# New-value gates of two GRU cells: from full-height halves to four quarters of the TensorE array

## The chip, the cores and the metric

The kernel runs on one core of a Trainium2 chip. The metric is device time of one execution in microseconds; the figure given is a median over runs. A profile of one execution, taken by the hardware profiler, shows every instruction of every engine. The engines are PE (TensorE, the matrix multiplier, whose weight loads are listed apart as PEld), DVE (VectorE), ACT (ScalarE), POOL (GpSimd) and SP (SyncE, which here issues the loads of the adjacency matrix).

## The reference

Four graph layers work on 3327 nodes with 64 features and a dense-stored adjacency matrix `adj` of 3327 x 3327 fp32. The layer that matters here is the first one: two gated cells one after the other, each with a product by `adj`.

```python
def _ggc(x, adj, W, wih, whh, bih, bhh):
    m = adj @ (x @ W)
    gi = m @ wih.T + bih
    gh = x @ whh.T + bhh
    i_r, i_z, i_n = jnp.split(gi, 3, axis=-1)
    h_r, h_z, h_n = jnp.split(gh, 3, axis=-1)
    r = jax.nn.sigmoid(i_r + h_r)
    z = jax.nn.sigmoid(i_z + h_z)
    n = jnp.tanh(i_n + r * h_n)
    return (1.0 - z) * n + z * x
...
h = jax.nn.relu(_ggc(x, adj, W1, wih1, whh1, bih1, bhh1))
return jax.nn.relu(_ggc(h, adj, W2, wih2, whh2, bih2, bhh2))
```

The new value `n` needs two products that cannot be added up in the matrix multiplier: the state part `h_n`, which is multiplied by `r`, and the message part `i_n`. For `r` and `z` the two parts are simply added.

The layers after it (a decayed neighbour sum, three hops with the squared matrix, two hops with tanh) are not touched.

## The kernel before

**Nodes and chunks.** The nodes are padded to 3328 and split into two halves `s = 0, 1` of 13 blocks of 128. Four chunks of nodes hold 3, 3, 3 and 4 of these blocks (of both halves): widths of 384, 384, 384 and 512 columns. Chunks 0 and 1 form group 0, chunks 2 and 3 group 1. A tile is 128 rows of the transposed adjacency matrix over the columns of one group, 768 or 896 KB, loaded by SP into one of 20 slots.

**Hops.** There are eight products by the matrix ("hops", k = 0 to 7). `alone(0, 0)` runs hop 0 for group 0 over all 26 tiles and counts the nonzero entries of every tile on the way (`count`, L598, from a mask that DVE makes at L517). Then `joint(1, 0)` runs hops 0 and 1 for group 1, `joint(0, 1)` hops 1 and 2 for group 0, and so on. `run()` writes out the order of all instructions by hand; the framework adds no reordering. The hop itself is L697: for each tile and chunk two matmuls, one for each half of the nodes, of 128 rows and 64 columns of weights. So the array is used as two column halves side by side, everywhere in the kernel.

**Tasks between.** Work that isn't a hop is a generator. It yields the time that it would like to let pass, and `spend` lets it go on when so much hop work has been issued; `take` may push other tasks on when no PSUM bank is free. `after_0` and `after_1` run the gated cell (`gru`) when a chunk's sum of hop 0 or 1 is complete.

**A cell.** `both[c]` holds two slabs of 128 partitions for a chunk. In slab `s` the partitions `upper(s)` hold the message `m` of half `s` (copied from PSUM by `evacuate_stacked`, L942 to L946), and the other 64 hold the state. `cells[:, cell, s, g]` holds the weights for slab `s` and gate `g`, stacked in the same order: g = 0 and 1 are `r` and `z`, with both parts; g = 2 is the state part of the new value, `nh`, with zeros in the message's rows; g = 3 is the message part, `ni`, with zeros in the state's rows. `gate(g)` (L1007) runs two matmuls of 128 rows and 64 columns, whose outputs are the two partition halves of one PSUM bank. ACT takes the sigmoids of `r` and `z` (L1012); DVE then forms `(nh + bias) * r` (L1017) and adds `ni` (L1019), ACT takes the tanh (L1028), and DVE blends (L1032 to L1034).

**The first cell's state part.** In the first cell the state is known from the start. `ahead_of_cell(c)` makes `nh` of chunk c with two matmuls (L217), and ACT copies it (L218) into half a tile slot (`rooms`), where it stays until `gru` reads it at L1017. `more_constants` calls it four times, 4 us of hop work apart, while the tiles of `alone(0, 0)` come in. `gru` then runs three gates in the first cell and four in the second.

Of the kernel before, what the change touches and what calls it, by code (L numbers as in the profile page):

```python
# [9 lines left out]
F32 = mybir.dt.float32  # L10
# [36 lines left out]
P = 128  # L47
# [5 lines left out]
CH = [(0, 3), (3, 6), (6, 9), (9, 13), (3, 5), (5, 6)]  # L53
NC = 4
PARTS = (4, 5)
CWM = 512
GROUPS = [(0, 1), (2, 3)]
# [39 lines left out]
def upper(n):  # L97
    return slice(n * D, (n + 1) * D)
# [3 lines left out]
def kernel(  # L102
# [9 lines left out]
    nc = tc.nc  # L112
# [16 lines left out]
    cells = const.tile([P, 2, 2, 4, D], F32, name="cells")  # L129
# [3 lines left out]
    both = [const.tile([P, 2, (b1 - b0) * P], F32, name=f"both{c}") for c, (b0, b1) in enumerate(CH[:NC])]  # L133
    both += [both[1][:, :, (CH[c][0] - CH[1][0]) * P:(CH[c][1] - CH[1][0]) * P] for c in PARTS]
    bcol = const.tile([P, NBIAS], F32, name="bcol")
# [29 lines left out]
    def unfold_cell(cell):  # L165

        n = 3 * D + (NBIAS if cell == 0 else 0)
        i, ps = take()
        for h in range(2):
            nc.tensor.matmul(ps[upper(h), :n], ident[:, :D], stage[:, 4 * D:4 * D + n], start=True, stop=True)  # L170
        v = ps[:, :3 * D].rearrange("p (g f) -> p g f", f=D)
        for h in range(2):
            nc.vector.tensor_copy(cells[upper(1 - h), cell, h, 0:3], v[upper(1 - h)])
        if cell == 0:
            nc.vector.tensor_copy(bcol, ps[:, 3 * D:n])
        give(i)
# [24 lines left out]
            nc.vector.tensor_copy(cells[upper(h), cell, h, 3], v[upper(h), 2])  # L201
        give(i)

    ahead = {}
    rooms = [None, None]

    def ahead_of_cell(c):

        finish(c)
        g = c // 2  # L210
        if rooms[g] is None:
            rooms[g] = Mask(sum(width(ch) for ch in GROUPS[g]))
        w0 = (CH[c][0] - CH[GROUPS[g][0]][0]) * P
        ahead[c] = rooms[g].view.rearrange("p s w -> p (s w)").bitcast(F32)[:, w0:w0 + width(c)]
        i, ps = take()
        for s in range(2):
            nc.tensor.matmul(ps[upper(1 - s), :width(c)], cells[:, 0, s, 2, :], both[c][:, s], start=True, stop=True)  # L217
        nc.scalar.copy(ahead[c], ps[:, :width(c)])  # L218
        give(i)

    def fold_hops():

        i, ps = take()
# [28 lines left out]
    def more_constants():  # L252
        nc.gpsimd.memset(cells, 0.0)
        for c in range(NC):
            for h in range(2):
                nc.gpsimd.memset(both[c][upper(h), h], 0.0)  # L256
        nc.gpsimd.memset(bd, 0.0)
        yield 4.5
        unfold_cell(0)
        yield 1.3  # L260

        full = work.tile([P, P], BF16, name="t2")
        nc.gpsimd.memset(full, -TWO7)
        nc.gpsimd.affine_select(out=tri, in_=full, pattern=[[-1, P]], compare_op=ALU.is_gt, fill=0.0,
                                base=0, channel_multiplier=1)
        nc.gpsimd.affine_select(out=tri, in_=tri, pattern=[[-1, P]], compare_op=ALU.not_equal, fill=TWO7 * TWO7,
                                base=0, channel_multiplier=1)
        nc.gpsimd.memset(tri[:, P - 1:P], 0.0)
        nc.gpsimd.memset(bitsb, BITS)
        nc.gpsimd.memset(lasty, 0.0)  # L270
        nc.gpsimd.memset(sel, 0.0)
        wide = work.tile([P, P], F32, name="t2")
        nc.gpsimd.memset(wide, 0.0)

        for h in range(2):
            nc.vector.tensor_tensor(sel[:, h, :NQ], ident[:, h * D:h * D + NQ],
                                    ident[:, h * D + LATE:h * D + LATE + NQ], ALU.add)
        for i, (bi, bh) in enumerate(((BI1, BH1), (BI2, BH2))):
            nc.vector.tensor_add(bsum[:, i], bcol[:, bi:bi + 2], bcol[:, bh:bh + 2])

        nc.vector.tensor_scalar(wide[0:D], wide[0:D], bcol[0:D, BL1:BL1 + 1], None, op0=ALU.add)
        yield 9.75
        i, ps = take()
        mm(ps[:, :D], wide, ident[:, :D])
        nc.vector.tensor_copy(brow[:, 3], ps[:, :D])
        give(i)
        yield 1.5
        have.add("row")
        yield from fold_cell(0)
        have.add(0)  # L290
        for c in range(NC):
            yield 4.0
            ahead_of_cell(c)
        yield 35.25
        load_cell(1)
        yield 20.0
        unfold_cell(1)
        yield from fold_cell(1)
        have.add(1)
        yield 10.4  # L300
        for h in range(2):
            nc.sync.dma_start(out=bd[upper(h), :, upper(h)], in_=weights[:, WL1:WL3])
            for i in range(2):
                nc.sync.dma_start(out=w3[upper(h), :, i], in_=weights[:, WL3 + (h + i) % 2:NW:2])
        yield 8.0
        nc.sync.dma_start(
            out=brow[:, 0:3],
            in_=bass.AP(tensor=bias_rows.tensor, offset=bias_rows.offset, ap=[[0, P], [D, 3], [1, D]]),
        )
        yield 21.0  # L310
        yield from fold_hops()
        have.add("hops")


    def blocks(c):
        return CH[c][1] - CH[c][0]

    def width(c):
        return blocks(c) * P

    def mm(out, lhsT, rhs, start=True, stop=True):


        for h in range(2):
            hs = slice(h * D, (h + 1) * D)
            nc.tensor.matmul(out[hs], lhsT[:, hs], rhs, start=start, stop=stop)  # L326
# [8 lines left out]
    def take(sums=False, either=True):  # L335


        either = either and not sums
        pool = idle_sums if sums else idle_temps
        if either and idle_sums and (not pool or released[idle_sums[0]] < released[pool[0]]):  # L340
            pool = idle_sums
        for c in list(tasks):
            if not pool and c not in running:
                advance(c)
        i = pool.popleft()
        return i, banks[i]

    def give(i):
        released[i] = max(released) + 1
        (idle_sums if i < 4 else idle_temps).append(i)  # L350
# [21 lines left out]
    def advance(c):  # L372
        running.add(c)
        try:
            tasks[c][1] = next(tasks[c][0])
        except StopIteration:
            del tasks[c]
        running.discard(c)
# [6 lines left out]
    def finish(c):  # L385
        while c in tasks:
            advance(c)
# [607 lines left out]
    def gru(acc, c, bi, bh, cell, pace=1.0):  # L995

        assert cell in have
        w = width(c)
        evacuate_stacked(acc, c, on_scalar=cell == 0)
        yield 0.8 * pace  # L1000
        at = dead.popleft()
        r, z, d = (slots[at].rearrange("p s w -> p (s w)")[:, i * CWM:i * CWM + w] for i in range(3))

        def gate(g):
            i, ps = take()
            for s in range(2):
                nc.tensor.matmul(ps[upper(1 - s), :w], cells[:, cell, s, g, :], both[c][:, s], start=True, stop=True)  # L1007
            return i, ps

        for g, v in enumerate((r, z)):  # L1010
            i, ps = gate(g)
            nc.scalar.activation(v, ps[:, :w], AF.Sigmoid, bias=bsum[:, cell, g:g + 1])  # L1012
            give(i)
        nh = None if cell == 0 else gate(2)
        ni = gate(3)
        yield 0.75 * pace
        nc.vector.scalar_tensor_tensor(r, ahead[c] if nh is None else nh[1][:, :w], bcol[:, bh + 2:bh + 3], r,  # L1017
                                       op0=ALU.add, op1=ALU.mult)
        nc.vector.tensor_tensor(r, r, ni[1][:, :w], ALU.add)  # L1019
        give(ni[0])  # L1020
        if nh is not None:
            give(nh[0])
        else:
            del ahead[c]
            if not any(ch in ahead for ch in GROUPS[c // 2]):
                rooms[c // 2].free()
        yield 1.2 * pace
        nc.scalar.activation(r, r, AF.Tanh, bias=bcol[:, bi + 2:bi + 3])  # L1028
        yield 0.8 * pace
        for s in range(2):  # L1030
            u = upper(1 - s)
            nc.vector.tensor_tensor(d[u], both[c][u, s], r[u], ALU.subtract)  # L1032
        nc.vector.tensor_tensor(d, d, z, ALU.mult)
        nc.vector.tensor_tensor(d, d, r, ALU.add)  # L1034
        if cell == 0:
            nc.vector.tensor_scalar(both[c][upper(0), 1], d[upper(0)], 0.0, None, op0=ALU.max)
            if c in GROUPS[1]:
                turned[c] = nodes(c)
                turn(turned[c], c, 1)
        yield 2.4 * pace  # L1040
        if cell == 0:
            nc.scalar.activation(both[c][upper(1), 0], d[upper(1)], AF.Relu)
            yield 0.6 * pace
        return at, d
# [181 lines left out]
```

## Time and profile before

| | |
|---|---|
| median of 3 runs | 685.08 us (684.77 to 685.13) |
| the profiled execution | 684.89 us, of which its span is 683.2 us |
| matmul instructions on PE | 4984 records, all of 64 weight columns |
| the ahead sums (L217) | 16 matmul records from 39.3 to 53.9 us |
| the gates (L1007) | 112 matmul records from 60.8 to 208.9 us |
| ACT's copies of the ahead sums (L218) | 4, of 479 to 587 ns |
| loads from memory | 201.30 MB, 295 GB/s on average over the span |

The span runs from the first to the last instruction, and the rest of the profiled execution's time lies around it. A matmul of fp32 data shows as two records, one for each pass, each with its own weight load. In a timeline several records of one kind are merged into one line: start, length from the first start to the last end, engine, line, operation, names, shapes, number, and in brackets how long the engine had been idle and what ended that. Matmul ends are modelled, so lengths overlap: what a matmul costs is the distance from its start to the start of what follows.

### The profile page before, as it was taken

To read this page: it belongs to the slowest core of one execution; us is meant where nothing else is said; L and a number is where in the kernel's file an instruction comes from. 1 tells how busy PE (TensorE), PEld (TensorE's weight loads), DVE (VectorE), ACT (ScalarE), POOL (GpSimd) and SP (SyncE) were. 2 spreads that over 40 slices of the span, in tenths; PEclk is the share of its full clock that TensorE was granted. 3 is DMA by queue.
4 is the path that set the end of the run, shared out by engine and by line. 5 is a ranking of instruction groups with operands and counts; after the bars stand their busy time and mean duration, and the time that the engine had idled before them with its cause. 6 is when DMAs were issued, how large, how long until landed. Compare 5 with 4: busy or idle time off the path is not lost.

```text
span 683.2 us, 12502 instructions
## 1 busy us (share of the span) xinstructions
PE 672.1 (98%) x4984; PEld 369.8 (54%) x4984; DVE 390.5 (57%) x839; ACT 272.4 (40%) x427; POOL 76.9 (11%) x115
## 2 busy tenths in 40 slices
PE   7999999999999999999999999999999999999997
PEld 5776444445558886566455554444444443344464
DVE  7954898739998999666542108215483893005101
ACT  1014000312148988999987009522366510000101
POOL 5400000002660504021000000000010000000000
PEclk9999999999999999999999999999999999999999
DMA  9999998299889615783999379954997399918991
GB/s 340 401 401 405 405 405 308 78 344 399 279 270 339 244 56 164 274 307 119 358 400 324 124 281 406 406 231 141 401 375 252 123 408 404 405 46 313 397 404 45
DMA packets 68693, 201.30 MB, mean 295 GB/s; under 512 B 7244, under 2 KB 8372, under 8 KB 68636
## 3 DMA queue, kind: packets, MB, share of 16 engines
q1 hardware_dynamic: 65724, 199.08, 78.0%
q10 hardware_dynamic: 736, 1.23, 0.5%
q8 instruction: 39, 0.64, 0.4%
q0 software_dynamic: 2176, 0.20, 0.2%
q14 instruction: 18, 0.15, 0.1%
HBM read 199.45 MB, written 0.85 MB: 293 GB/s over the span
## 4 chain that ended last, share of the span: by engine, by line
PE 94%; DVE 2%; POOL 2%; issue 0%; DMA 0%; ACT 0%; DVEq 0%; ACTq 0%; POOLq 0%
PE sum L697 81%; PE temp L326 5%; PE temp L1007 2%; PE sum L326 1%; PE temp L598 1%; PE sum L1007 1%; PE temp L886 1%; PE temp L611 1%; POOL both L256 1%; DVE e L573 0%; POOL st L966 0%; DMA xs<-in_x 0%; DVE adj L517 0%; DVE st L963 0%; DVE y L962 0%
## 5 line engine op out<-in xcount | busy, mean ns | idle before, releaser
L697 PE MATMUL sum<-adj,y 128*64 128x384 f32 (+3 forms) x3016 | 533.0, 501 | 0.0
L697 PEld LDWEIGHTS sum<-adj,y 128*64 128x64 f32 x3016 | 242.7, 137 | 241.4 <-issue 151.3
L481 ACT ACTIVATE adj<-adj 128x768 f32<-128x768 f32 (+1 forms) x169 | 138.1, 890 | 27.0 <-DMA adj<-in_adjT 13.7
L517 DVE TENSOR_SCALAR adj<-adj 128x768 f16<-128x768 f32 (+2 forms) x156 | 86.2, 594 | 9.8 <-DMA adj<-in_adjT 6.7
L697 PE MATMUL sum<-e,both 128*64 128x384 bf16 (+1 forms) x624 | 73.9, 339 | 0.0
L575 ACT ACTIVATE e<-temp,bitsb 128x384 int16<-128x384 f32 (+1 forms) x113 | 63.6, 605 | 13.2 <-PE temp L326 11.3
L942 ACT COPY both<-sum 64x384 f32<-64x384 f32 (+3 forms) x17 | 8.1, 478 | 145.4 <-PE sum L697 145.3
L483 DVE TENSOR_TENSOR adj<-adj 128x768 f32<-128x768 f32 (+1 forms) x39 | 37.7, 1013 | 42.9 <-DMA adj<-in_adjT 31.8
L946 DVE COPY both<-sum 64x384 f32<-64x384 f32 (+3 forms) x11 | 6.2, 561 | 97.9 <-ACT both L942 96.7
L937 DVE STREAM_TRANSPOSE y<-t 32x96 f32<-32x96 f32 (+1 forms) x128 | 35.6, 278 | 40.8 <-ACT t L922 39.2
L966 POOL TENSOR_TENSOR st<-st,mhalf 128x6 f32<-128x6 f32 (+1 forms) x16 | 25.5, 1592 | 296.9 <-DVE st L964 296.9
L697 PEld LDWEIGHTS <-both 128*64 128x64 bf16 x624 | 44.6, 110 | 13.3 <-issue 3.5
L523 POOL DMA_DIRECT2D adj<-totals x52 | 32.0, 617 | 165.4 <-DVE adj L512 128.6
L326 PE MATMUL temp<-adj,tri 128*64 128x384 bf16 (+1 forms) x316 | 49.0, 341 | 0.1
L573 DVE TENSOR_SCALAR e<-temp 128x384 int16<-128x384 f32 (+1 forms) x45 | 27.7, 618 | 19.1 <-ACT e L575 12.0
L326 PEld LDWEIGHTS <-tri 128*64 128x64 bf16 x416 | 30.3, 110 | 13.7 <-issue 7.8
L915 DVE STREAM_TRANSPOSE both<-y 32x96 f32<-32x96 f32 (+1 forms) x128 | 35.6, 278 | 2.5
L512 DVE SCALAR_TENSOR_TENSOR adj<-adj,adj 128x896 f16<-128x896 f32 x26 | 28.4, 1092 | 0.9
L922 ACT ACTIVATE t<-sum,hopcol 128x384 f32<-128x384 f32 (+1 forms) x8 | 4.9, 608 | 51.8 <-PE sum L697 49.0
L575 ACT ACTIVATE e<-sum,bitsb 128x384 int16<-128x384 f32 (+1 forms) x35 | 20.5, 593 | 5.4 <-PE sum L326 3.8
L598 PE MATMUL temp<-adj,behind 128*64 128x384 f16 x104 | 18.4, 327 | 2.1 <-DVE adj L517 1.9
L326 PE MATMUL sum<-adj,tri 128*64 128x384 bf16 (+1 forms) x100 | 18.5, 335 | 0.9 <-DVE e L573 0.7
(153 smaller groups left out, 360.0 us busy)
## 6 DMA issues: line engine op xcount, KB each, us to landing
adj<-in_adjT SPq DMA_DIRECT2D x130, 768.0 KB, 8.7
adj<-in_adjT SPq DMA_DIRECT2D x104, 896.0 KB, 12.9
xs<-in_x ACTq DMA_DIRECT2D x1, 448.0 KB
adj<-totals POOLq DMA_DIRECT2D x26, 3.0 KB, 4.6
adj<-totals POOLq DMA_DIRECT2D x26, 3.5 KB, 2.9
out<-xs ACTq DMA_DIRECT2D x1, 256.0 KB
xs<-in_x ACTq DMA_DIRECT2D x1, 192.0 KB, 3.1
xs<-in_x SPq DMA_DIRECT2D x1, 192.0 KB
```

The costliest lines, as they stand in the source:

```text
L326: nc.tensor.matmul(out[hs], lhsT[:, hs], rhs, start=start, stop=stop)
L481: nc.scalar.activation(sq, v, AF.Square)
L483: nc.vector.tensor_tensor(sq, v, v, ALU.mult)
L512: nc.vector.scalar_tensor_tensor(t.mask.ones, t.view()[:, 1], 0.0, t.mask.ones, op0=ALU.not_equal, op1=ALU.add)
L517: nc.vector.tensor_scalar(to[:rows, half], t.view()[:rows, half], 0.0, None, op0=ALU.not_equal)
L523: nc.gpsimd.dma_start(out=t.mask.view[P - 1:P], in_=totals[t.g][t.q:t.q + D + 1:D, :])
L573: nc.vector.tensor_scalar(wide[:, s], ps[:, :w], BITS, 0.0, op0=ALU.add, op1=ALU.max)
L575: nc.scalar.activation(wide[:, s], ps[:, :w], AF.Relu, bias=bitsb)
L697: nc.tensor.matmul(acc[h][1][h * D:(h + 1) * D, :w], yq[h], rhs[h], start=first and n == 0, stop=last and n == len(terms) - 1)
L915: nc.vector.transpose(to[at:at + 32, :, q], h[q * 32:(q + 1) * 32, :, s, f * 32:(f + 1) * 32])
L937: nc.vector.transpose(yk[q * 32:(q + 1) * 32, :, s, f * 32:(f + 1) * 32], v[at:at + 32, :, q])
L966: nc.gpsimd.tensor_tensor(st[:, 3, :n], st[:, 2, :n], mhalf[:, :n], ALU.pow)
```

## The change

The function `ahead_of_cell` and its rooms go, with the four calls. `more_constants` lets 16 us pass in their place, as before. In `gru` both cells now make `nh` and `ni` at the same place, in two PSUM banks, with four matmuls that take only the 64 rows that hold nonzero weights:

```diff
-        for c in range(NC):
-            yield 4.0
-            ahead_of_cell(c)
+        yield 16.0
...
-        nh = None if cell == 0 else gate(2)
-        ni = gate(3)
+        nh, ni = take(), take()
+        for s in range(2):
+            for (_, ps), g, rows in ((nh, 2, upper(1 - s)), (ni, 3, upper(s))):
+                nc.tensor.matmul(ps[upper(1 - s), :w], cells[rows, cell, s, g, :], both[c][rows, s],
+                                 start=True, stop=True)
         yield 0.75 * pace
-        nc.vector.scalar_tensor_tensor(r, ahead[c] if nh is None else nh[1][:, :w], bcol[:, bh + 2:bh + 3], r,
+        nc.vector.scalar_tensor_tensor(r, nh[1][:, :w], bcol[:, bh + 2:bh + 3], r,
                                        op0=ALU.add, op1=ALU.mult)
         nc.vector.tensor_tensor(r, r, ni[1][:, :w], ALU.add)
         give(ni[0])
-        if nh is not None:
-            give(nh[0])
-        else:
-            del ahead[c]
-            if not any(ch in ahead for ch in GROUPS[c // 2]):
-                rooms[c // 2].free()
+        give(nh[0])
```

The four matmuls use four different quarters of the array. For s = 0, `nh` takes rows 64 to 127 and `ni` rows 0 to 63, both into columns 64 to 127; for s = 1 the rows are exchanged, and the columns are 0 to 63. `nh` goes to one bank and `ni` to the other.

In the order of instructions, the eight matmuls of L217 and the four copies of L218 leave, and each of the eight calls of `gru` has the block of four quarter matmuls in place of one gate (first cell) or of two (second cell). SP issues the second cell's weights one tile load later than before; POOL's order is unchanged.

More of the change, by code (lines that the diff above doesn't have):

```diff
@@ L202, in fold_cell @@
         give(i)
[L204 to L219, printed above, removed]
     def fold_hops():
```

## The prediction

> **What bounds the kernel.** I read the page's busy line and its chain of waits first, then busy time by window, then the timeline around the edited lines.
>
> ```profile
> PE 672.1 (98%) x4984; PEld 369.8 (54%) x4984; DVE 390.5 (57%) x839; ACT 272.4 (40%) x427; POOL 76.9 (11%) x115
> ...
> PE 94%; DVE 2%; POOL 2%; issue 0%; DMA 0%; ACT 0%; DVEq 0%; ACTq 0%; POOLq 0%
> ```
>
> TensorE is busy 98% of the span and 94% of the chain. Matmul time given or taken reaches the end nearly one for one, except where something else would become last. The windows look for that:
>
> ```profile
> 34.00:51.00 17.00, 17.00 (x134) 13.36 (x130) 9.62 (x22) 2.60 (x5) 0.00 (x0) 1.00 1.03 401
> 51.00:60.00 9.00, 9.00 (x67) 6.86 (x65) 4.67 (x10) 0.59 (x1) 0.00 (x0) 1.00 1.03 402
> 60.00:74.00 14.00, 14.00 (x102) 7.71 (x100) 8.05 (x15) 8.20 (x15) 0.00 (x0) 1.00 1.03 405
> 118.00:130.00 12.00, 12.00 (x68) 5.32 (x66) 7.19 (x20) 5.48 (x10) 0.00 (x0) 1.00 0.00 1
> 148.00:165.00 17.00, 16.89 (x107) 8.55 (x105) 12.24 (x21) 4.27 (x8) 2.78 (x5) 1.00 1.03 395
> 198.00:212.00 14.00, 14.00 (x114) 7.80 (x111) 10.89 (x20) 10.19 (x21) 1.88 (x3) 1.00 0.95 310
> ```
>
> The columns are stretch, length, busy time of PE, weight load, DVE, ACT and POOL, granted clock, DMA share and GB/s. The state sums ahead of the first cell lie at 39 to 54 us, the first cell's gates at 61 to 66 and 121 to 129, the second's at 150 to 164 and 200 to 209. PE is full in all of them at clock 1.00. In the first three the DMA is full as well (share 1.03), so there a saving on PE may only uncover a late tile.
>
> **Price of a gate.** In the timeline of PE:
>
> ```profile
> 160.44 1.08 PE L1007 MATMUL temp<-both,cells 128*64 128x512 f32 x4
> 161.30 1.08 PE L1007 MATMUL sum<-both,cells 128*64 128x512 f32 x4
> 162.16 1.08 PE L1007 MATMUL temp<-both,cells 128*64 128x512 f32 x4
> 163.02 1.08 PE L1007 MATMUL sum<-both,cells 128*64 128x512 f32 x4
> 163.88 0.87 PE L697 MATMUL sum<-adj,y 128*64 128x384 f32 x4
> ```
>
> One gate is four records: two halves of 64 columns, each with two fp32 passes. The gates start 0.86 us apart at 512 wide. At 384 the ahead gate at 39.35 is followed by the next group at 39.99, so it costs 0.645. One gate over all four chunks is 3 x 0.645 + 0.86 = 2.80 us.
>
> **Part 1, the ahead sums go.** This removes 2.80 us of PE at L217 and four ACT copies (0.48 to 0.59 us each, in front of which ACT sat idle for 13 us, so they give nothing). How much of the 2.80 reaches the end? The DVE and PE timelines around the last tile of the first sweep:
>
> ```profile
> 56.58 1.03 DVE L517 TENSOR_SCALAR adj<-adj 128x768 f16<-128x768 f32 x2 [0.94 <-DMA adj<-in_adjT]
> 58.52 1.03 DVE L517 TENSOR_SCALAR adj<-adj 128x768 f16<-128x768 f32 x2 [0.91 <-DMA adj<-in_adjT]
> ```
>
> ```profile
> 58.94 0.59 PE L598 MATMUL temp<-adj,behind 128*64 128x384 f16 x4
> 59.26 1.56 PE L697 MATMUL sum<-adj,y 128*64 128x384 f32 x8
> 60.55 0.43 PE L598 MATMUL temp<-adj,behind 128*64 128x384 f16 x2
> ```
>
> DVE makes a tile's mask as soon as the tile lands, and each time it has waited some 0.9 us for the DMA: a tile lands every 1.95 us. PE spends 1.29 us on a tile (59.26 to 60.55) and 0.325 on its count (58.94 to 59.26), 1.615 in all. Left alone it would catch up by 0.33 us per tile. That it shows full here only means that it runs behind the landings: by 1.95 us at the tile masked at 40.63 (used at 42.58), by 0.74 at the last one. So the ahead sums mostly fill time in which PE would wait for tiles. Without them PE starts the last tile at its landing, 58.40, or a few hundredths later. The gain is 59.26 - 58.46 = **0.8 us**, not 2.8.
>
> Does the 0.8 survive? What follows starts from the end of that tile and moves along: four ACT copies, the table load (1.28 us), the sigmoids, DVE's chain, whose copy at L1079 ends at 73.45 and releases the first weights of hop 1 at 73.50. The next landing that could bite is tile 31, at 69.69; PE first uses it at 70.5, so its slack is also 0.8. I take 0.8 in full; the lower end is 0 (the chain doesn't move), and nothing here can lose.
>
> **Part 2, new-value gates in quarters.** Per chunk, the first cell had one full-height gate (ni) at this place and now has nh and ni; the second cell had both. The new form issues four matmuls of 64 rows by 64 columns, each on its own quarter. Call q the time of the four, and S what entering and leaving the form costs. If the quarters run at once, q is one gate. Then the second cell saves 2.80 us and the first neither gains nor loses. If row halves take turns, q is two gates: the second cell saves nothing and the first pays 2.80.
>
> No row shows the form: all matmul records of the trace are 128*64. The nearest is how the two column halves share the array. At 61.46 the second gate's first record starts before the first gate's last (61.61), whose half had waited for an ACT copy. Different column quarters thus run as independent streams, and I take the same for row quarters. The Trainium skill (TensorE: Matmul & The Clock Gate, Part 3) reports row and column tiles starting some 4 ns apart, so by it q is one gate plus 12 ns. Ends for q: one gate, two gates; I take one.
>
> Now S. The weight rows of the same stretch:
>
> ```profile
> 161.30 0.20 PEld L1007 LDWEIGHTS sum<-both,cells 128*64 128x64 f32 x2 [0.23 <-issue]
> 161.73 0.20 PEld L1007 LDWEIGHTS temp<-both,cells 128*64 128x64 f32 x2 [0.23 <-issue]
> ```
>
> Each pair of loads starts with a matmul and serves the next one, so loads and the emptying of the array cost nothing today. By the trace alone, S is 0. But every matmul has one shape here, and **a rule of the skill speaks against the change**: TensorEngine Tiling, Key Properties, says that changing the tiling mode, as against merely the tile, drains TensorE. Each block now changes mode twice. An estimate of the price from rows: a 384-wide fp32 pass is recorded for 0.486 us while its stream takes 0.3225, so 0.164 us of emptying becomes visible. Then a load must precede the first matmul: in the run of L886 at 74.20 load and following matmul are 0.055 us apart. That is 0.22 per change, 0.44 for two, and 0.105 more because the column halves run 0.105 us out of step and the earlier must wait: S = 0.55 us. With eight blocks (four chunks, two cells) this is 4.4 us.
>
> By the trace's habit: -2.8 - 0.8 = -3.6 us. By the rule: -3.6 + 4.4 = **+0.8 us**. I take the rule, because it states this case and the trace is silent. Ends for S: 0, and 0.85 if the full weight record (0.137) and both halves' offset show at each change.
>
> Where S falls matters little. Every block has waiting L697 matmuls behind it on PE, and those are the bound. The first cell pays 4 x 0.55 - 0.8 = +1.4; the second 4 x 0.55 - 2.8 = -0.6. L1017's operand now ends with ni, not long before it; for the first chunk that is hidden under the table load.
>
> **Small edits, at nothing.** L1017 in the first cell reads PSUM, not SBUF: 618 ns either way in the rows of that line. It holds a fourth PSUM bank there, as the second cell already did. SP issues the second cell's weights one tile load later; they are used over 20 us after. The ahead sums no longer hold halves of tile slots; after the first 8 us PE's list of waits shows none for a DMA, so deeper loading gives nothing.
>
> **The sum.** The profiled execution took 684.89 us (span 683.2, 1.7 around it). 684.89 + 0.8 = 685.7; it lies 0.19 below the median of the runs shown, so on the median's scale 685.9.
>
> **Rivals.** *No drain.* The array tracks its quarters one by one, S is 0 to 0.25. For it: the column halves run independently. Against: the skill's sentence. Time: 685.1 - 3.6 + 8 x 0 to 0.25 = 681.5 to 683.5. Chance 0.26.
>
> *Rows take turns.* Place: the pair nh, ni. The skill (TensorEngine Tiling, Gotcha 1) says that row tiles can't access one PSUM bank simultaneously. Here nh's upper half comes from the lower rows and its lower half from the upper rows, both into one bank, in different partitions. If the bank is guarded whole, q becomes two gates: -0.8 + 2.8 = +2.0 without a drain (687.1), +6.4 with it (691.5). A gate over all eight blocks is 5.6 us; with my S, q = 1.1 gates already brings +1.4 us, from where it can be told from no change. Chance 0.22.
>
> *Drain as priced*, chance 0.52, from S = 0.3 (683.9) to 0.85 (688.3). It includes the case that the 0.8 of part 1 is not had (686.7).
>
> **From cases to numbers.** About 0.2% (1.4 us) is what a measurement can tell from no change: 683.7 and 686.5. The first rival is faster, 0.26, and 0.01 of the drain case falls there. Of the drain case 0.30 lies within and 0.21 above; with 0.22 for rows in turn, slower is 0.43. The likeliest case's own range is 683.9 to 688.3. Leaving out the best corner of the first rival (about 0.08) and the dearest of the second (about 0.1), the range is 681.8 to 689.3.
>
> **What would show it.** In the profile after: no L217; the last tile of the first sweep starting on PE within 0.1 us of its landing; four 64*64 records starting nearly together. Around each block, a gap of 0.2 to 0.3 us between the last record's stream and the first weight load, on both sides. The forecast is wrong if the next L697 group follows a 384-wide block 0.65 us after its start (no drain), or 1.3 us after with two records at a time (rows in turn).

## The result, and the profile after

The changed kernel takes 683.26 us (median of 10 runs, 683.05 to 683.32), the kernel before 684.95 in the same comparison (684.69 to 685.23): a ratio of 0.9975, 95% interval 0.9967 to 0.9983. It is 1.7 us faster. The forecast was 0.8 us slower: the change went the other way, and the time lies below the range given for the likeliest case (683.9 to 688.3).

The page of the changed kernel, its busy line and the chain:

```profile
PE 669.4 (98%) x4984; PEld 354.5 (52%) x4984; DVE 389.7 (57%) x839; ACT 270.5 (40%) x423; POOL 76.6 (11%) x115
...
PE 91%; DVE 3%; DMA 3%; POOL 2%; issue 0%; ACT 0%; DVEq 0%; ACTq 0%; POOLq 0%
```

PE is still the bound. New in the chain is 3% of DMA: nearly all of it is the stretch from 43.4 to 58.1 us of the first sweep, where PE has caught up with the tiles. The windows of the first sweep say the same; PE was full there before, and now it waits for 0.47 us of 9.00:

```profile
34.00:51.00 17.00, 17.00 (x137) 13.08 (x133) 9.94 (x23) 1.16 (x2) 0.00 (x0) 1.00 1.03 401
51.00:60.00 9.00, 8.53 (x58) 3.30 (x54) 4.48 (x9) 0.97 (x3) 0.00 (x0) 1.00 1.03 402
```

The same stretch in the timelines of DVE and of PE:

```profile
56.19 1.03 DVE L498 TENSOR_SCALAR adj<-adj 128x768 f16<-128x768 f32 x2 [0.93 <-DMA adj<-in_adjT]
58.15 1.03 DVE L498 TENSOR_SCALAR adj<-adj 128x768 f16<-128x768 f32 x2 [0.93 <-DMA adj<-in_adjT]
```

```profile
54.15 1.51 PE L678 MATMUL sum<-adj,y 128*64 128x384 f32 x8
55.49 0.49 PE L579 MATMUL temp<-adj,behind 128*64 128x384 f16 x4
56.11 1.51 PE L678 MATMUL sum<-adj,y 128*64 128x384 f32 x8
57.45 0.49 PE L579 MATMUL temp<-adj,behind 128*64 128x384 f16 x4
58.07 1.51 PE L678 MATMUL sum<-adj,y 128*64 128x384 f32 x8
```

PE starts a tile every 1.96 us, the pace of the loads, though its own work on a tile is 1.6. It starts the last tile at 58.07, 0.05 after the trace shows it landed (58.02), and the mask follows.

A quarter block stands in the timeline of PE like this (start, length, names, rows*columns of weights, number of records):

```profile
160.88 1.05 PE L988 MATMUL temp<-both,cells 128*64 128x512 f32 x4
161.86 1.09 PE L998 MATMUL temp<-both,cells 64*64 64x512 f32 x8
162.88 0.87 PE L678 MATMUL sum<-adj,y 128*64 128x384 f32 x4
```

and its weight loads like this:

```profile
161.86 0.21 PEld L998 LDWEIGHTS temp<-both,cells 64*64 64x64 f32 x8 [0.81 <-issue]
162.88 0.20 PEld L678 LDWEIGHTS sum<-adj,y 128*64 128x64 f32 x4 [0.81 <-issue]
```

Two gates of 512 columns stood here for 1.72 us; now both take 1.02 to the next start. All four quarters run at once. And no weight load runs ahead over a change of form: the loads start together with the first matmuls at 161.86 and again at 162.88, while at 161.30 of the kernel before each load served the next matmul. In the other blocks, where the records stand apart, the four first passes start 0.007 us apart:

```profile
64.46 0.53 PE L998 MATMUL sum<-both,cells 64*64 64x384 f32 x1
64.47 0.53 PE L998 MATMUL temp<-both,cells 64*64 64x384 f32 x1
64.48 0.53 PE L998 MATMUL sum<-both,cells 64*64 64x384 f32 x1
64.48 0.53 PE L998 MATMUL temp<-both,cells 64*64 64x384 f32 x1
64.84 0.48 PE L998 MATMUL sum<-both,cells 64*64 64x384 f32 x1
...
65.27 2.15 PE L678 MATMUL sum<-adj,y 128*64 128x512 f32 x10
```

What a block pays can be added up from such rows; all eight are alike within 0.01 us. (A pass of 384 columns streams for 0.3225 us; the later of the two column halves counts.) From the end of the last full-height stream to the first quarter: 0.09. The first pass streams 0.05 longer (64.46 to 64.84 is 0.374), and it is the one whose weights were not loaded ahead. The four are 0.02 apart. From the end of the last quarter's stream to the next full-height matmul: 0.09. And that one's first pass is 0.05 longer again. Together **0.30 us**.

Where the time went, by when the same matmul of a hop starts in the two profiled executions (after less before, mean of the two column halves, which in the kernel before run up to 0.4 us out of step):

| where | difference, us |
|---|---|
| last tile of the first sweep | -1.2 |
| after the first cell of group 0 | -0.65 |
| after the first cell of group 1 | +0.2 |
| after the second cell of group 1 | -0.9 |
| after the second cell of group 0 | -1.5 |
| from 267 us to the end | -1.6 |

The first sweep and the second cell gain, the first cell pays. The last 0.15, at 267 us, lies far from the edit and isn't explained.

### The profile page after: what moved, and what is told of

Read it like the earlier page. It is cut to its first block, busy times and chain, and to the rows that moved or that the text cites. A ratio compares the mean times of both kernels' runs of the same rounds, so it can differ in the third digit from the quotient of the medians.

```text
span 681.6 us, 12505 instructions
## 1 busy us (share of the span) xinstructions
PE 669.4 (98%) x4984; PEld 354.5 (52%) x4984; DVE 389.7 (57%) x839; ACT 270.5 (40%) x423; POOL 76.6 (11%) x115
## 4 chain that ended last, share of the span: by engine, by line
PE 91%; DVE 3%; DMA 3%; POOL 2%; issue 0%; ACT 0%; DVEq 0%; ACTq 0%; POOLq 0%
PE sum L678 79%; PE temp L307 5%; DMA adj<-in_adjT 2%; PE sum L307 2%; PE temp L988 1%; PE temp L867 1%; PE temp L592 1%; PE temp L579 1%; POOL both L239 1%; PE sum L988 1%; PE temp L998 1%; DVE e L554 0%; DMA xs<-in_x 0%; POOL st L947 0%; DVE adj L498 0%
## 5 line engine op out<-in xcount | busy, mean ns | idle before, releaser
L678 PEld LDWEIGHTS sum<-adj,y 128*64 128x64 f32 x3016 | 235.4, 137 | 249.7 <-issue 167.2
L678 PEld LDWEIGHTS <-both 128*64 128x64 bf16 x624 | 42.8, 110 | 14.5 <-issue 3.6
L307 PE MATMUL temp<-adj,tri 128*64 128x384 bf16 (+1 forms) x314 | 47.1, 341 | 0.1
L307 PEld LDWEIGHTS <-tri 128*64 128x64 bf16 x416 | 28.7, 110 | 14.7 <-issue 8.6
L493 DVE SCALAR_TENSOR_TENSOR adj<-adj,adj 128x896 f16<-128x896 f32 x26 | 28.4, 1092 | 0.9
L579 PE MATMUL temp<-adj,behind 128*64 128x384 f16 x104 | 17.0, 327 | 2.1 <-DVE adj L498 1.9
```

The source lines that it names most:

```text
L493: nc.vector.scalar_tensor_tensor(t.mask.ones, t.view()[:, 1], 0.0, t.mask.ones, op0=ALU.not_equal, op1=ALU.add)
L678: nc.tensor.matmul(acc[h][1][h * D:(h + 1) * D, :w], yq[h], rhs[h], start=first and n == 0, stop=last and n == len(terms) - 1)
```

## The experiments

All are timed in five rounds beside the kernel before, whose median was 684.9 each time.

**Quarters in the second cell alone.** The first cell keeps its ahead sums.

```diff
-        nh = None if cell == 0 else gate(2)
-        ni = gate(3)
+        if cell == 0:
+            nh, ni = None, gate(3)
+        else:
+            nh, ni = take(), take()
+            for s in range(2):
+                for (_, ps), g, rows in ((nh, 2, upper(1 - s)), (ni, 3, upper(s))):
+                    nc.tensor.matmul(ps[upper(1 - s), :w], cells[rows, cell, s, g, :], both[c][rows, s],
+                                     start=True, stop=True)
```

> Quarters in the second cell alone; the first cell keeps its ahead sums and its three full-height gates. Cheap switch (a block costs some 0.30 us over one gate, plus what the two column halves are out of step): the second cell's stretches were 2.0 us shorter in the changed kernel's trace, so 2.0 us under before. Switch as predicted (0.55): 4 x 0.55 - 2.80 = 0.6 us under. Gain of the change from the first sweep alone, quarters worth nothing: the same as before.

Measured: 683.70 us, ratio 0.9982 (0.9975 to 0.9989): 1.2 under before. The quarters pay for themselves where they replace two gates. Saved 2.80 less 1.2 leaves 1.6 for four blocks, 0.40 each: more than the 0.30 of the rows, less than the predicted 0.55. The last set of experiments shows where the other 0.4 went: not into the blocks.

**Neither ahead sums nor quarters.** From the changed kernel:

```diff
-        nh, ni = take(), take()
-        for s in range(2):
...
+        nh, ni = gate(2), gate(3)
```

> No ahead sums and no quarters: both cells run four full-height gates. The first cell gains a gate at its place (+2.80 us), the first sweep loses the ahead sums. First sweep worth 1.2 us, as the two traces show: 1.6 us over before. Worth 0.8, as predicted (the rest of the trace's 1.2 being loads that happened to land earlier): 2.0 over. Ahead sums free in the sweep: 2.8 over.

Measured: 686.12 us, ratio 1.0017 (1.0011 to 1.0024): 1.2 over before. Four full-height gates at the first cell's place cost 2.80 (by the starts of hop matmuls in its trace, 1.28 in group 0 and 1.50 in group 1); so taking the ahead sums away gave 1.6, twice the predicted 0.8. In its trace, PE's row for the last tile:

```profile
58.05 1.51 PE L678 MATMUL sum<-adj,y 128*64 128x384 f32 x8
```

That tile had landed at 58.01. In the kernel with quarters in the second cell alone, which has the ahead sums, it landed at 58.01 as well, and the rows of DVE and PE are:

```profile
56.35 1.03 DVE L517 TENSOR_SCALAR adj<-adj 128x768 f16<-128x768 f32 x2 [0.58 <-PE temp L598]
58.14 1.03 DVE L517 TENSOR_SCALAR adj<-adj 128x768 f16<-128x768 f32 x2 [0.76 <-PE temp L598]
```

```profile
57.77 1.56 PE L697 MATMUL sum<-adj,y 128*64 128x384 f32 x8
59.06 0.59 PE L598 MATMUL temp<-adj,behind 128*64 128x384 f16 x4
59.38 1.56 PE L697 MATMUL sum<-adj,y 128*64 128x384 f32 x8
```

With ahead sums PE works at its own pace of 1.61 us to the very end and is 1.37 us behind the landing; without, 0.04. The sweep is worth 59.38 - 58.05 = 1.3 us. In the profiled execution from which the prediction took its 0.8, the last tile had landed at 58.40, 0.4 later than in these two. PE there was still behind the tiles, so that execution was no slower for it, but it hid 0.4 us of what an earlier PE can gain.

The other 0.3 us arrives at 148 us: ACT's copy of the second cell's first sum (L942) starts 0.44 us after the last record of that sum before, and 0.10 after it in this kernel and in the changed one. All traces of this case fall into these two groups: 0.43 to 0.45 in the five kernels with all four ahead sums, 0.10 to 0.11 in the seven with two or none. In the five the copy starts when the first record of the next chunk's sum has ended. So it does follow from the ahead sums; why the copy is released sooner without them is not shown.

**A change of form with nothing beside it.** In the kernel before, the second cell's state part takes 64 rows, the message part stays full height.

```diff
-        nh = None if cell == 0 else gate(2)
+        nh = None
+        if cell:
+            nh = take()
+            for s in range(2):
+                rows = upper(1 - s)
+                nc.tensor.matmul(nh[1][rows, :w], cells[rows, cell, s, 2, :], both[c][rows, s], start=True, stop=True)
         ni = gate(3)
```

> Kernel before, but in the second cell the state part nh runs in 64 rows by 64 columns and the message part ni stays full height. Nothing runs beside it that did not before; only the array's form changes twice in each of four blocks. Cheap switch: 4 x 0.30 = 1.2 us over before, up to 1.8 with the halves out of step. Switch as predicted: 4 x 0.55 = 2.2 us over. No cost of a switch as such: the same as before.

Measured: 686.12 us, ratio 1.0018 (1.0010 to 1.0026): 1.2 over before, 0.30 for each of the four blocks. In PE's timeline:

```profile
162.19 1.03 PE L1007 MATMUL sum<-both,cells 128*64 128x512 f32 x4
163.15 1.07 PE L1019 MATMUL temp<-both,cells 64*64 64x512 f32 x4
164.15 1.08 PE L1007 MATMUL sum<-both,cells 128*64 128x512 f32 x4
```

The starts are 0.96 and 1.00 apart where gates of this width stood 0.86 apart, and the next first pass is 0.05 longer: 0.29 us. By the starts of hop matmuls its four blocks cost 0.31, 0.30, 0.31 and 0.32. The matmuls stream as long as before, only the form changes. So changing form costs time by itself, as the Trainium skill has it (TensorEngine Tiling, Key Properties), and it costs 0.15 us each time.

**Ahead sums for group 1 only.** Quarters in the second cell, and in the first cell where there is no ahead sum.

```diff
         for c in range(NC):
             yield 4.0
-            ahead_of_cell(c)
+            if c in GROUPS[1]:
+                ahead_of_cell(c)
...
-        nh = None if cell == 0 else gate(2)
-        ni = gate(3)
+        if c in ahead and cell == 0:
+            nh, ni = None, gate(3)
+        else:
...
```

> Quarters in the second cell for all chunks and in the first cell for group 0; ahead sums for group 1 alone, with full-height gates there. Cheap switch: the changed kernel's first cell in group 1 was 0.94 us longer than before, which goes, while two ahead sums (1.5 us) come back into the first sweep, mostly hidden: 2.3 us under before (0.6 under the changed kernel). Switch as predicted: -0.6 (second cell) + 1.1 (group 0) - 0.8 = 0.3 us under before. If any ahead sum costs its full time in the sweep: 1.1 us under before.

Measured: 682.85 us, ratio 0.9969 (0.9957 to 0.9981): 2.1 under before, the lowest median of all. It is 0.4 under the changed kernel, though the ranges of their runs touch (682.53 to 683.10 against 683.05 to 683.32) and the intervals overlap. PE's rows at the end of the first sweep:

```profile
56.60 1.51 PE L698 MATMUL sum<-adj,y 128*64 128x384 f32 x8
57.95 0.49 PE L599 MATMUL temp<-adj,behind 128*64 128x384 f16 x4
58.57 1.51 PE L698 MATMUL sum<-adj,y 128*64 128x384 f32 x8
```

PE starts the last tile 0.04 after its landing, but here the tile was half a microsecond late (58.53). The last kernel below has the same first sweep; there the tile landed at 57.96, and PE's row is

```profile
58.20 1.56 PE L698 MATMUL sum<-adj,y 128*64 128x384 f32 x8
```

0.24 behind the landing. So two ahead sums, 1.5 us of PE, fit into the time in which PE would wait for tiles but for some 0.2 us. Four leave it 1.3 to 1.4 us behind.

**Gates issued later; quarters first.** Two attempts at the time lost beyond 0.30. In four of the eight blocks, where a cell starts, the second half's copy comes some 0.5 us after the first's, so the two column halves reach the block out of step. The first edit (also made to the kernel with ahead sums for group 1) is one number, the second moves the block ahead of r and z, with nh ahead of ni in it.

```diff
         evacuate_stacked(acc, c, on_scalar=cell == 0)
-        yield 0.8 * pace
+        yield 1.4 * pace
```

> The changed kernel with the gates issued one hop unit later after the two copies of the message (1.4 in place of 0.8 us of hop work). If the two column halves being out of step at the entry is what costs beyond the switch (0.43 to 0.60 us in four of the eight blocks, half of the array each time: 1.0 us in all), both copies are done before the gates reach TensorE and up to 1.0 us comes back: 682.3. If the out-of-step halves cost nothing, the same as the changed kernel, 683.3, or a little slower because the chain of the cell starts 0.6 us later.

> Ahead sums for group 1 alone, quarters elsewhere, and the later gates as well. If the out-of-step halves cost: 682.85 less up to 0.8 (three of the four such blocks are left): 682.1. If not: 682.9.

> The changed kernel with the quarter block ahead of the gates r and z, and nh ahead of ni within it: nh needs no message and may start before the copies land, and the entry comes straight after the hop, where the halves are in step. If waiting for the copies at the entry is what costs: up to 1 us under the changed kernel. If the wait only moves into the block (ni still waits for the second copy, with the other quarters done): the same, 683.3, or slower, since the sigmoids come 0.9 us later.

Measured: 689.09 us (ratio 1.0066, 1.0054 to 1.0078), 690.08 (1.0077, 1.0063 to 1.0092) and 683.75 (0.9983, 0.9976 to 0.9990). The later gates don't answer the question, for other waits swamp it. In the list of PE's waits of the changed kernel with later gates (engine, line, waited for, total us, times, longest) are, and were not in the changed kernel's:

```profile
PE temp L307 <- DVE adj L1003: 2.1, 1, 2.1
PE sum L678 <- DVE y L974: 1.9, 1, 1.9
...
PE temp L592 <- DVE adj L493: 1.8, 2, 1.6
```

These are 5.8 us in all, as much as the kernel lost: with 0.6 us of delay at the head of a cell's chain PE comes to its end before DVE is there. The chain had been hidden by a narrow margin. In the kernel with the quarters first, ni of the second half starts 0.3 to 0.6 us after the others in four blocks: the wait moves into the block, and the sigmoids come later. It is 0.5 slower than the changed kernel.

**In step and out of step, apart.** Quarters in the second cell alone, once only for chunks 0 and 3 and once only for 1 and 2. The same pair of chunks, 0 and 3, was then tried in the kernel with ahead sums for group 1.

```diff
         if cell == 0:
             nh, ni = None, gate(3)
+        elif c not in (0, 3):
+            nh, ni = gate(2), gate(3)
         else:
```

> Quarters only in the second cell and there only for chunks 0 and 3, whose column halves end together (0.03 us apart) before the block; the rest as in the kernel before. Saved: 0.645 + 0.86 us, paid: two blocks at 0.30. Both theories (halves out of step cost, or don't): 0.9 us under before. With the switch as predicted (0.55): 0.4 under.

> Quarters only in the second cell and there only for chunks 1 and 2, whose column halves end 0.58 to 0.60 us apart before the block. Saved: 2 x 0.645, paid: two blocks at 0.30. If being out of step costs nothing: 0.7 us under before. If the earlier half's wait is lost (half of the array for 0.6 us, twice): 0.1 under, which can't be told from no change.

> Ahead sums for group 1 alone, quarters in the first cell for group 0 and in the second cell for chunks 0 and 3. If being out of step costs: within 0.2 us of the kernel that has quarters in all chunks of the second cell (682.85). If it doesn't: 0.7 us over that, 683.5.

Measured: 684.10 us (0.9989, 0.9982 to 0.9995), 684.39 (0.9992, 0.9984 to 1.0000) and 683.13 (0.9976, 0.9966 to 0.9985). In step gave 0.8 of the 0.9 expected. Out of step gave 0.5: nearer to 0.7 (being out of step costs nothing) than to 0.1. The third lies 0.3 over the kernel with quarters for all four chunks, between the two expectations. The intervals are half a microsecond wide each way, so that the medians alone don't settle it; the traces do. Of the blocks of the form change with nothing beside it, those of chunks 1 and 2 are out of step by 0.6 us, and they cost 0.31 and 0.32 like the others. Being out of step costs nothing there.

What is missing is time in which PE waits for DVE. In the kernel with quarters in the second cell alone, after the block of chunk 2:

```profile
158.54 1.09 DVE L512 SCALAR_TENSOR_TENSOR adj<-adj,adj 128x896 f16<-128x896 f32 x1
```

```profile
159.26 0.80 PE L611 MATMUL temp<-adj,behind 128*64 128x448 f16 x4
159.68 0.11 PEld L611 LDWEIGHTS <-behind 128*64 128x64 f16 x1 [0.31 <-issue]
159.87 0.84 PE L697 MATMUL sum<-adj,y 128*64 128x384 f32 x4
```

and in the kernel before:

```profile
158.35 1.09 DVE L512 SCALAR_TENSOR_TENSOR adj<-adj,adj 128x896 f16<-128x896 f32 x1
159.48 0.54 PE L611 MATMUL temp<-adj,behind 128*64 128x448 f16 x3
159.80 0.87 PE L697 MATMUL sum<-adj,y 128*64 128x384 f32 x4
```

L611 counts two tiles from masks that DVE makes. DVE ends the second mask at 159.63, and the second count starts at 159.68, 0.23 us later than it would straight after the first. (The profile names no releaser for this wait. In the list above, where it is longer, the same two lines stand as L592 and L493.) In the kernel before PE came later, and the mask was ready. So the next hop starts 0.07 after that of the kernel before, where it had been 0.12 after it ahead of the block: of the 0.345 saved little is left. After chunk 3 the same happens to the matmuls of L326. DVE's last step of the cell and the start of L326, here and then in the kernel before:

```profile
169.17 0.69 DVE L1040 TENSOR_TENSOR adj<-adj 128x512 f32<-128x512 f32 x1
170.01 1.15 PE L326 MATMUL temp<-ident,adj 128*64 128x64 f32 x32
```

```profile
169.54 0.69 DVE L1034 TENSOR_TENSOR adj<-adj 128x512 f32<-128x512 f32 x1
170.38 1.15 PE L326 MATMUL temp<-ident,adj 128*64 128x64 f32 x32
```

Both times L326 starts 0.15 after DVE's step has ended. Before, PE's own stream ended only then; here it had ended 0.13 earlier. The two waits make 0.36 of the missing 0.4; the 0.13 alone is about what chunks 0 and 3 miss, the 0.23 alone about what chunks 1 and 2 miss. The changed kernel shows both. This is read from the traces; no run took the waits away.

## Why the prediction was wrong

**The step that failed is the size of S**, "S = 0.55 us. With eight blocks (four chunks, two cells) this is 4.4 us". The mechanism was right: a change of form stops PE, and loads don't run ahead across it. Its price is 0.30 us for a block, 2.4 for eight. The sum took 0.164 us of visible emptying per change from the length of a record; the rows show 0.09 between the streams. The 0.055 for a load was near what is seen (0.05). The 0.105 for halves out of step was charged to every block; four of the eight enter in step, and where the others could be told apart they cost no more.

**Part 1 was right in kind and half its size in fact**: "59.26 - 58.46 = **0.8 us**, not 2.8". PE does wait for the tiles afterwards, and a good part of the 2.80 was idle time filled. But 58.46 came from one execution whose last tile was late by 0.4 us; the sweep gives 1.3, and 0.3 more came at 148 us, which no step foresaw. The gain then passed the DVE chain and the landing of tile 31, as assumed.

**The waits for DVE stood at nothing.** "Where S falls matters little", since waiting hop matmuls were taken as the bound behind every block. Behind two blocks of the second cell DVE was the bound as soon as PE came earlier: 0.36 us of the gain went there.

**q = one gate** holds: the four quarters of a pass start within 0.02 us (0.007 apart, where the prediction had some 0.004), and a block costs one gate and S. The rival with rows taking turns is out, and with it the fear for the PSUM bank: nh's two halves come from different rows into one bank, in different partitions, at the same time. For this case the sentence that the rival quoted does not hold.

**The sum with measured terms**: -2.8 (second cell's gate) - 1.6 (first sweep and what came of it) + 8 x 0.30 + 0.36 (waits for DVE) = -1.6; measured -1.7. Against the forecast of +0.8, S accounts for -2.0, part 1 for -0.8 and the waits for +0.36. By the medians, the second cell gains 1.2 (1.6 less the waits), and the first with its sweep some 0.4 (683.70 less 683.26), since 1.6 saved is set against 1.2 for its four blocks.

**The choice between rule and row** was the wrong frame. The rule gave the sign of a cost and no figure; the figure was an estimate of mine from lengths that are modelled. The break-even lay at 0.45 us a block, and the estimate's own ends (0 to 0.85) lay on both sides of it. The rival "no drain", at S up to 0.25, named 681.5 to 683.5 and so held the measured time. That was luck: S is above its bound, and what it lacked in cost the larger gain of part 1 made up for.

## What to carry to other kernels

Half-size matmuls that can run side by side in quarters of the array are worth a change of form when what they save exceeds 0.30 us for entering and leaving it; here a 384-wide fp32 gate (0.645) does. What is saved reaches the end only if the engine that PE waits for next is ready as early: here DVE took back 0.36 of it. Work put into the gaps of a stage that waits for loads is free only up to the size of the gaps: compare when PE starts the last tile with when it landed, in more than one execution. Landings moved by 0.4 to 0.6 us between executions with the same sweep, and twice here a late tile made a gap look smaller or a fit look better than it was. When a cost has a break-even inside its bounds, the sign isn't known, and the smallest kernel that pays only this cost (a form change with nothing beside it) is the run that tells it.

## What was not expected of the hardware

The change of the array's form costs 0.15 us each way: 0.09 without a stream and 0.05 in the first pass, whose weights are no longer loaded ahead. It is the same in all eight blocks, at 384 and 512 columns, and with two quarters in use as with four. And the whole cell hangs on a margin of under a microsecond: issuing its gates 0.6 us of hop work later cost 5.8 us against the changed kernel.
